# Attention and mixture-of-experts layer on one core: row scatters ahead of the sums of states in GpSimd's order, and one power instead of two for the second layernorm and the mean square

## The chip, the cores and the metric

The kernel runs on one core of a Trainium2 chip. Every time is device time in microseconds (us) of one execution. The engines of the core work side by side, each through its own instructions in its own order, and wait for one another by semaphores: TensorE (PE, matmuls, with PEld for its weight loads), VectorE (DVE), ScalarE (ACT), GpSimd (POOL), and SyncE (SP), which only issues transfers. The kernel is compared by the median time of its runs.

## The reference

The input x has 16 sequences of 512 tokens with 128 numbers each, all float32. Cut to what matters:

```python
q, k, v = silu(x @ Wq), silu(x @ Wk), x @ Wv            # 16 heads of 8
q, k = lrpe(q, theta), lrpe(k, theta)                   # [t*cos, t*sin]: 16 per head
energy = einsum('bhnd,bhmd->bhnm', q, k) * tril         # causal, no softmax
out = einsum('bhnm,bhmd->bhnd', energy, v) @ Wo
out = layernorm(out * sigmoid(x @ G1 @ G2)) * gamma + beta
x1 = layernorm(x + out)                                 # the second layernorm

xn = x1 * rsqrt(mean(x1 * x1) + eps)                    # the mean square, for the router only
probs = softmax(xn @ router_w.T)                        # 8 experts, the best 2 of each token
# each expert takes its first 1280 tokens: (silu(t @ rg) * (t @ ru)) @ rd, weighted, added back
ffn = silu(x1 @ sg) * (x1 @ su) @ sd + routed
return layernorm(x1 + ffn)
```

`x1` has variance var / (var + LN_EPS) over its 128 numbers and mean 0, where var is the variance before the second layernorm. So the mean square of `x1` follows from var alone, and both factors, (var + LN_EPS)^-0.5 and (var / (var + LN_EPS) + RMS_EPS)^-0.5, can be formed from it.

## The kernel before

**Layout.** Tokens lie on the 128 partitions. A chunk is 128 tokens; there are 64 chunks `t`, four to a sequence `b` (so `t = 4b + c`). Everything on PE, ACT, DVE and POOL runs in the order in which the program writes it: no engine takes an instruction ahead of another of its own.

**The first stage** (lines 788 to 832) is a loop over steps `t` = -2 to 64. Attention without softmax is computed by chunks with a running state, in a software pipeline. Step `t` emits, in this order:

- `project(t+2)`: one projection into the PSUM tile `pq` (L418, L421). ACT empties `pq` with SiLU into `qk` (L425, L427), tanh into `gate` (L433) and four copies into `vpad` (L441). DVE multiplies `qk` with cosines and sines into `hat` (L445).
- a piece of the shared feed-forward network of an earlier sequence, if one is ready: matmul `pg` (L137) and SiLU `sl` on ACT (L139), or matmul `pu` (L150) and product `h` on DVE (L151), or half of a down projection `pd` (L160) with a sum on DVE (L165).
- `turn_over(t+1)`: PE transposes `hat` into `pt` (L458); ACT copies it out as `kT`, `q2`, `qT` (L460 to L467). Another shared piece.
- `advance(turns)`: the next stage of `after(b)`, below.
- `energies(t)`: 32 small matmuls `pe` (L505), masked by four DVE products `et` (L513).
- `values(t-1)`: matmuls into `pout` from the states (L530) and from `et` (L538); ACT copies `pout` into `oT` (L544).
- `remember(t+1)`: matmuls `pst` (L479). DVE masks each into `add` (L488) and POOL adds it to the state (L490). A middle state and a last state come out of each chunk. They are read by `values` two and three steps later.
- if there are rows to send, up to two row scatters: first a tiny product `beat` on POOL (L740) which reads the `oT` column that ACT has just written, so that the scatter does not start before that; then one `scatter` (L723), an indirect DMA that GpSimd prepares, and a second one.
- `advance(turns)` again, then routing steps.

Most PSUM tiles of this stage come from one pool, `ps_w`, with four buffers in turn. A new tile takes the buffer of the tile four before it, so a matmul can wait for the engine that empties that older tile. The output projection `po` often takes the buffer of the `pq` that was filled in the same step.

**`after(b)`** finishes a sequence. It is a generator, and each `advance` runs it to its next `yield`, so its stages are half a step apart, or more: `po` (L553) and the POOL sum `x_sb + bet` (L554); the gate product `o` (L557); the first layernorm's statistics and its power `rstd` on POOL (L113); `w` in two stages (L565, L570); the statistics of `w` (L105, L107) and, with `rstd_of`, `ve = var + eps` on DVE (L111) and its power `r2` on POOL (L113); an empty stage; then `nb = -mean * r2` on DVE (L580), half of the normalised rows `x1` on ACT (L584, `normed_rows(0, 1)`), and for the mean square three small DVE operations on 128x4 numbers (L591, L592, L593) and a second power on POOL into `rms` (L594). Then follow the other half of the rows, their transpose, and the router's logits.

**Routing** runs three times (`route`, after sequences 5, 11 and 15). It reads `rms` and leaves 2 rows to scatter for each token chunk, 128 scatters in all. 52 of them go out in the loop, the others in the tail behind it (lines 838 to 856), each behind a `beat` on the newest `h`.

**The second stage** (lines 999 to 1066) runs the eight experts and the last layernorm. There POOL prepares only the scatters of the results (L934) and the powers of the last layernorm (L113).

Of the kernel before, what the change touches and what calls it, by code (L numbers as in the profile page):

```python
# [10 lines left out]
F32 = mybir.dt.float32  # L11
I32 = mybir.dt.int32
AF = mybir.ActivationFunctionType
ALU = mybir.AluOpType
# [5 lines left out]
P = 128  # L20
B, N, D = 16, 512, 128
NC = N // P
T = B * N
NT = T // P
# [5 lines left out]
LN_EPS = 1e-5  # L30
RMS_EPS = 2.0 ** -23
# [16 lines left out]
def tile_kernel(  # L48
# [20 lines left out]
    nc = tc.nc  # L69
# [20 lines left out]

    x1T = keep.tile([P, T], F32, name="x1T")
    base = x1T.rearrange("p (t d) -> p t d", d=D)
    rms = keep.tile([P, NT], F32, name="rms")
    logits = keep.tile([P, NT, E], F32, name="logits")
    idx = keep.tile([P, 2, NT], I32, name="idx")
    count = keep.tile([P, E], F32, name="count")
# [12 lines left out]
    def rstd_of(var, n, eps):  # L109
        ve = small.tile([P, n], F32, tag="ve", name="ve")  # L110
        nc.vector.tensor_scalar(ve, var, eps, None, ALU.add)  # L111
        r = small.tile([P, n], F32, tag="rstd", name="rstd")
        nc.gpsimd.tensor_tensor(r, ve, neghalf[:, :n], ALU.pow)  # L113
        return r
# [80 lines left out]
    with ExitStack() as ph:  # L195
# [351 lines left out]
        def after(b):  # L547

            mine = slice(b * NC, b * NC + NC)
            oT, gate, x_sb = oTs.pop(b), gates.pop(b), xs.pop(b)  # L550
            po = ps_w.tile([P, NC, D], F32, tag="w", name=f"po_{b}")
            for c in range(NC):
                nc.tensor.matmul(po[:, c, :], oT[:, ts(c, P)], wo_sb, start=True, stop=True)  # L553
            nc.gpsimd.tensor_tensor(x_sb, x_sb, bet.unsqueeze(1).to_broadcast([P, NC, D]), ALU.add)  # L554
            yield
            o = wk1.tile([P, NC, D], F32, tag="o", name=f"o_{b}")
            nc.vector.scalar_tensor_tensor(o, gate, 1.0, po, ALU.add, ALU.mult)  # L557
            yield
            mv = small.tile([P, NC, 2], F32, tag="mv", name="mv")
            ln_stats(o, mv, NC)  # L560
            r = rstd_of(mv[:, :, 1], NC, LN_EPS)
            yield
            w = wk1.tile([P, NC, D], F32, tag="w", name=f"w_{b}")
            for c in range(NC):
                nc.vector.scalar_tensor_tensor(  # L565
                    w[:, c, :], o[:, c, :], mv[:, c, 0:1], gam, ALU.subtract, ALU.mult
                )
            yield
            for c in range(NC):
                nc.vector.scalar_tensor_tensor(  # L570
                    w[:, c, :], w[:, c, :], r[:, c : c + 1], x_sb[:, c, :], ALU.mult, ALU.add
                )
            yield
            mv2 = small.tile([P, NC, 2], F32, tag="mv2", name="mv2")
            ln_stats(w, mv2, NC)
            r2 = rstd_of(mv2[:, :, 1], NC, LN_EPS)
            yield
            yield
            nb = small.tile([P, NC], F32, tag="nb", name="nb")
            nc.vector.scalar_tensor_tensor(nb, mv2[:, :, 0], -1.0, r2, ALU.mult, ALU.mult)  # L580

            def normed_rows(*chunks):
                for c in chunks:
                    nc.scalar.activation(  # L584
                        x1[:, b * NC + c, 0:D], w[:, c, :], AF.Identity, bias=nb[:, c : c + 1], scale=r2[:, c : c + 1]
                    )

            normed_rows(0, 1)

            sq = small.tile([P, NC], F32, tag="sq", name="sq")  # L590
            nc.vector.tensor_tensor(sq, r2, r2, ALU.mult)  # L591
            nc.vector.tensor_tensor(sq, sq, mv2[:, :, 1], ALU.mult)  # L592
            nc.vector.tensor_scalar(sq, sq, RMS_EPS, None, ALU.add)  # L593
            nc.gpsimd.tensor_tensor(rms[:, mine], sq, neghalf[:, :NC], ALU.pow)  # L594
            yield
            normed_rows(2, 3)
            yield
            px1 = ps_w.tile([P, N], F32, tag="w", name=f"px1_{b}")
            for c in range(NC):
                nc.tensor.transpose(px1[:, ts(c, P)], x1[:, b * NC + c, 0:D], ident)  # L600
            nc.scalar.copy(x1T[:, ts(b, N)], px1)
            yield "narrow"
            plg = ps_w.tile([P, P], F32, tag="w", name=f"plg_{b}")
            for c in range(NC):
                nc.tensor.matmul(
                    plg[32 * c : 32 * c + 32, :], rw_sb, x1T[:, ds(b * N + c * P, P)], start=True, stop=True
                )
            lg = wk1.tile([P, P], F32, tag="lg", name=f"lg_{b}")
            nc.scalar.copy(lg, plg)
            yield  # L610
            yield
            plt = ps_w.tile([P, NC, 32], F32, tag="w", name=f"plt_{b}")
            nc.tensor.transpose(plt.rearrange("p c e -> p (c e)"), lg, ident)
            nc.vector.tensor_copy(logits[:, mine, :], plt[:, :, 0:E])
            normed.add(b)
# [120 lines left out]
        def scatter_behind(column=None):  # L736

            if scatters:
                if column is not None:
                    nc.gpsimd.tensor_tensor(beat, column, neghalf[:, 0:1], ALU.mult)  # L740
                scatter(*scatters.pop(0))
# [6 lines left out]
        def advance(gens, slot=None):  # L748

            for g in list(gens):  # L750
                if told.get(id(g)) == slot:
                    told[id(g)] = next(g, gens)
                    if told[id(g)] is gens:
                        gens.remove(g)
                        del told[id(g)]
# [32 lines left out]
        with tc.manual_schedule(engines=ORDERED):  # L788
            for t in range(-2, NT + 1):
                coming, here, left = 0 <= t + 2 < NT, 0 <= t < NT, 0 <= t - 1 < NT  # L790
                stopped("wait")
                beginning(t)
                if coming:
                    if (t + 2) % NC == 0 and 2 <= (t + 2) // NC + 1 < B:
                        load_xT((t + 2) // NC + 1)
                        load_x((t + 2) // NC + 1)
                    project(t + 2)
                if t == 0:
                    nc.vector.tensor_scalar(wo_sb, wo_sb, 0.5, None, ALU.mult)
                if t == 2:  # L800
                    nc.sync.dma_start(sg_sb, sg)
                    nc.sync.dma_start(su_sb, su)
                    nc.sync.dma_start(sd_sb, sd.rearrange("(c p) d -> p c d", p=P))
                shared(t)
                sprinkle(t, 2)
                if 0 <= t + 1 < NT:
                    turn_over(t + 1)
                shared(t)
                advance(turns)
                if here:  # L810
                    energies(t)
                if stopped("exp"):
                    sprinkle(t, 1)
                if left:
                    values(t - 1)
                if 0 <= t + 1 < NT:
                    remember(t + 1)
                if left:

                    scatter_behind(oTs[(t - 1) // NC][:, ds((t - 1) % NC * P, 1)])  # L820
                    scatter_behind()
                advance(turns, "narrow")
                advance(turns)
                sprinkle(t, 3)
                beginning_done(t)
                if left and (t - 1) % NC == NC - 1:
                    b = (t - 1) // NC
                    turns.append(after(b))
                    ready[b] = t + (6 if b else 10)
                    for b0, b1 in groups:  # L830
                        if b == b1 - 1:
                            todo.append((b, route(b0, b1)))

            t, over, waited = NT + 1, 12, 0

            zero = vpads[0].rearrange("p a b d -> p (a b d)")[:, 0:N]
            nought(zero, N)
            while turns or todo or scatters or fills or over:
                if not (turns or todo or scatters or fills):
                    over -= 1  # L840
                shared(t)

                waited = waited + 1 if todo and told.get(id(todo[0][1])) == "wait" else 0
                if waited > 1:
                    stopped("wait")
                if stopped("exp"):
                    sprinkle(t, 1)
                if t % 2 == 0:
                    advance(turns, "narrow")
                    advance(turns)  # L850
                sprinkle(t, 3)
                if t % 2 == 0:
                    scatter_behind(latest[0])
                if t % 4 == 1 and fills:
                    fill(fills.pop(0))
                t += 1
# [256 lines left out]
```

## Time and profile before

| | us |
|---|---|
| median of 12 runs | 854.61 (852.68 to 857.12) |
| the profiled execution: its time | 854.15 |
| the profiled execution: span from first to last instruction | 852.4 |
| PE busy | 815.0 (96%) |
| DVE busy | 537.5 (63%) |
| ACT busy | 413.8 (49%) |
| POOL busy | 360.0 (42%) |
| POOL row scatters L723, 128 | 128.6, 1004 ns each |
| POOL powers L113, 45 | 48.6, 1080 ns each |
| POOL sums of states L490, 96 | 43.9, 458 ns each |
| POOL powers of the mean square L594, 16 | 16.6, 1040 ns each |

A row of the groups reads: line, engine, operation, output <- inputs, shapes, count, then busy time in all, mean ns of one, and the idle time of that engine just before them. A row of the timeline reads: start, duration (of all of the instructions merged into the row), engine, line, operation, tiles, and in brackets the idle time of the engine before it and who ended it. A row of the waits reads: who waited for whom, us in total, times, longest. Matmuls are pipelined and their ends are modelled, so a PE that is shown as busy can still lose a tenth of a microsecond between two matmuls; where that matters, starts are compared.

The first stage with its tail takes the span up to some 510 us. Within it the four chunks of a sequence take about 22 us, and in most of it PE shows no idle time, while DVE is busy for 17 to 18 us of each 22.

### The profile page before, as it was taken

The numbers are of one execution on the slowest core, as the hardware profiler recorded it, in microseconds if no ns is written. First come the engines' busy times: TensorE is split into PE (matmuls) and PEld (weight loads), VectorE is DVE, ScalarE is ACT, GpSimd is POOL, SyncE is SP. The second block draws the span as 40 slices with busy tenths as digits, with TensorE's granted clock in tenths as the row PEclk, the third lists the DMA queues.
The fourth block names the chain that finished last, engine by engine and source line by source line (L and its number), as shares of the span: only waits on it lengthen the run. The fifth ranks groups of instructions, "written<-read, shape, count | busy, mean of one in ns | idle before, by whom it ended". The sixth has DMA issues, their size and how long they took to land. (4 is left out here: it accounts for less than half of the span.)

```text
span 852.4 us, 25793 instructions
## 1 busy us (share of the span) xinstructions
PE 815.0 (96%) x10288; PEld 556.7 (65%) x10288; DVE 537.5 (63%) x1695; ACT 413.8 (49%) x1342; POOL 360.0 (42%) x512
## 2 busy tenths in 40 slices
PE   6899999989999999999999999999999999999996
PEld 4666667656766865755666666776777667765564
DVE  7688887889988788975433334443434443278864
ACT  5666776675676567534222221333333333323455
POOL 2233333322466776686766660433343333401110
PEclk9999999999999999999999999999999999999998
DMA  6011111110111110057000014213331110056512
GB/s 202 22 35 35 35 33 35 34 34 17 39 55 57 59 48 21 29 201 261 26 13 7 1 31 140 82 36 93 94 97 50 64 62 25 31 160 180 144 49 63
DMA packets 66395, 57.55 MB, mean 68 GB/s; under 512 B 6180, under 2 KB 55132, under 8 KB 66274
## 3 DMA queue, kind: packets, MB, share of 16 engines
q1 hardware_dynamic: 59474, 44.95, 17.2%
q0 software_dynamic: 6656, 10.69, 3.8%
q8 instruction: 81, 1.33, 0.6%
q14 instruction: 40, 0.33, 0.1%
q10 hardware_dynamic: 144, 0.26, 0.1%
HBM read 32.62 MB, written 26.48 MB: 69 GB/s over the span
## 5 line engine op out<-in xcount | busy, mean ns | idle before, releaser
L723 POOL DMA_INDIRECT xg_dram<-x,idx x128 | 128.6, 1004 | 40.5 <-issue 35.2
L934 POOL DMA_INDIRECT y_dram<-y,to x80 | 77.6, 970 | 158.0 <-ACT y L932 158.0
L151 DVE TENSOR_TENSOR h<-sl,pu 128x512 f32<-128x512 f32 x128 | 87.7, 685 | 84.6 <-PE pu L150 56.4
L139 ACT ACTIVATE sl<-pg 128x512 f32<-128x512 f32 x128 | 75.5, 593 | 118.1 <-PE pg L137 112.5
L150 PE MATMUL pu<-x1T,su_sb 128*128 128x512 f32 x256 | 130.9, 593 | 0.8 <-ACT sl L139 0.8
L137 PE MATMUL pg<-x1T,sg_sb 128*128 128x512 f32 x256 | 131.4, 595 | 0.0
L160 PE MATMUL pd<-sd_sb,h 128*128 128x128 f32 x1024 | 122.8, 276 | 4.4 <-DVE x1T L165 4.4
L1026 DVE TENSOR_TENSOR eh<-esl,peu 128x512 f32<-128x512 f32 (+1 forms) x96 | 57.5, 598 | 109.8 <-PE peu L1023 109.8
L160 PEld LDWEIGHTS pd<-sd_sb,h 128*128 128x128 f32 x1024 | 119.1, 192 | 11.2 <-issue 5.7
L113 POOL TENSOR_TENSOR rstd<-ve,neghalf 128x4 f32<-128x4 f32 x45 | 48.6, 1080 | 125.9 <-DVE ve L111 121.0
L928 PEld LDWEIGHTS ped<-rd,eh 128*128 128x128 f32 x640 | 84.0, 192 | 24.6 <-issue 22.5
L490 POOL TENSOR_TENSOR state<-state,add 128x128 f32<-128x128 f32 x96 | 43.9, 458 | 130.3 <-DVE add L488 127.7
L513 DVE TENSOR_TENSOR et<-pe,causal 128x256 f32<-128x256 f32 x256 | 90.2, 413 | 9.9 <-PE pe L505 9.8
L1021 PE MATMUL peg<-xgT,rg 128*128 128x512 f32 (+1 forms) x192 | 84.6, 522 | 0.0
L1023 PE MATMUL peu<-xgT,ru 128*128 128x512 f32 (+1 forms) x192 | 84.4, 521 | 0.0
L928 PE MATMUL ped<-rd,eh 128*128 128x128 f32 x640 | 84.3, 275 | 0.0
L1025 ACT ACTIVATE esl<-peg 128x512 f32<-128x512 f32 (+1 forms) x96 | 50.5, 526 | 55.0 <-PE peg L1021 52.3
L150 PEld LDWEIGHTS pu<-x1T,su_sb 128*128 128x128 f32 x256 | 45.7, 190 | 45.1 <-issue 39.0
L932 ACT ACTIVATE y<-ped,wt 128x128 f32<-128x128 f32 x80 | 29.4, 367 | 84.6 <-PE ped L928 84.6
L137 PEld LDWEIGHTS pg<-x1T,sg_sb 128*128 128x128 f32 x256 | 44.4, 191 | 36.9 <-issue 34.8
L418 PE MATMUL pq<-W,xT 128*128 128x384 f32 x128 | 61.0, 560 | 4.9 <-ACT qT L467 2.6
L445 DVE TENSOR_TENSOR hat<-qk,cst_tok 128x512 f32<-128x512 f32 x64 | 44.9, 702 | 26.5 <-ACT qk L427 26.4
(176 smaller groups left out, 1258.7 us busy)
## 6 DMA issues: line engine op xcount, KB each, us to landing
y_dram<-vpad SPq DMA_DIRECT2D x16, 512.0 KB, 7.0
y<-y_dram SPq DMA_DIRECT2D x32, 256.0 KB, 3.2
xT<-xt SPq DMA_DIRECT2D x15, 384.0 KB, 2.9
xg<-xg_dram SPq DMA_DIRECT2D x8, 660.0 KB, 4.4
x<-x SPq DMA_DIRECT2D x16, 256.0 KB, 3.3
o<-res SPq DMA_DIRECT2D x15, 256.0 KB, 2.3
xg_dram<-x,idx POOLq DMA_INDIRECT x128, 2.3
rg<-rg SPq DMA_DIRECT2D x8, 256.0 KB, 3.6
```

Source lines behind the costliest of these rows:

```text
L137: nc.tensor.matmul(pg, sg_sb[:, ts(i, P)], seq, start=True, stop=True)
L139: nc.scalar.activation(sl, pg, AF.Silu)
L150: nc.tensor.matmul(pu, su_sb[:, ts(i, P)], seq, start=True, stop=True)
L151: nc.vector.tensor_tensor(h[i // half][:, i % half, :], h.pop(("s", i)), pu, ALU.mult)
L160: nc.tensor.matmul(pd, h[k][:, i - k * half, ts(c, P)], sd_sb[:, i, :], start=(i == 0), stop=(i == IS // P - 1))
L418: nc.tensor.matmul(pq[:, :, 0:24], xts[b][:, c, 0:P], W[:, 0:384].rearrange("p (h n) -> p h n", n=24), start=True, stop=True)
L513: nc.vector.tensor_tensor(et.rearrange("p s i n -> p (s i) n"), pes[a, half].rearrange("p s i n -> p (s i) n"), causal.unsqueeze(1).to_bro ...
L723: i = nc.gpsimd.indirect_dma_start(out=xg_dram[:, :], out_offset=bass.IndirectOffsetOnAxis(ap=idx[:, k, t : t + 1], axis=0), in_=x1[:, t, ...
L928: nc.tensor.matmul(pd, h[:, i, ts(c, P)], got[e][2][:, i, :], start=(i == 0), stop=(i == IR // P - 1))
L934: i = nc.gpsimd.indirect_dma_start(out=y_dram[:, :], out_offset=bass.IndirectOffsetOnAxis(ap=to[:, at : at + 1], axis=0), in_=y, in_offset ...
L1021: nc.tensor.matmul(pg[:, :n], rg_sb[:, ts(i, P)], xgTs[e][:, ds(o0, n)], start=True, stop=True)
L1023: nc.tensor.matmul(pu[:, :n], ru_sb[:, ts(i, P)], xgTs[e][:, ds(o0, n)], start=True, stop=True)
```

## The change

Two things are changed.

1. In `after(b)` the second layernorm's stage forms both arguments at once: `ve[:, 0] = var + LN_EPS`, then `inv = 1 / ve[:, 0]`, `inv = inv * var`, `ve[:, 1] = inv + RMS_EPS`, on DVE, and one POOL power of 128x2x4 numbers writes both factors into the kept tile `norms`. `rms` is its second half. The three small DVE operations and the power that stood behind `nb` one step later are gone.
2. In the loop, the two scatters with their `beat` stand in front of `remember(t+1)` instead of behind it. PE, ACT, DVE and SP keep their order under this. On POOL the order of a step becomes `beat`, scatter, scatter, sums of states, instead of sums of states, `beat`, scatter, scatter.

```diff
-    rms = keep.tile([P, NT], F32, name="rms")
+    norms = keep.tile([P, 2, NT], F32, name="norms")
+    rms = norms[:, 1]
...
             ln_stats(w, mv2, NC)
-            r2 = rstd_of(mv2[:, :, 1], NC, LN_EPS)
+
+            ve = small.tile([P, 2, NC], F32, tag="ve2", name="ve2")
+            nc.vector.tensor_scalar(ve[:, 0], mv2[:, :, 1], LN_EPS, None, ALU.add)
+            inv = small.tile([P, NC], F32, tag="sq", name="inv")
+            nc.vector.reciprocal(inv, ve[:, 0])
+            nc.vector.tensor_tensor(inv, inv, mv2[:, :, 1], ALU.mult)
+            nc.vector.tensor_scalar(ve[:, 1], inv, RMS_EPS, None, ALU.add)
+            nc.gpsimd.tensor_tensor(
+                norms[:, :, mine], ve, neghalf[:, : 2 * NC].rearrange("p (k c) -> p k c", k=2), ALU.pow
+            )
+            r2 = norms[:, 0, mine]
             yield
             yield
...
             normed_rows(0, 1)
-
-            sq = small.tile([P, NC], F32, tag="sq", name="sq")
-            nc.vector.tensor_tensor(sq, r2, r2, ALU.mult)
-            nc.vector.tensor_tensor(sq, sq, mv2[:, :, 1], ALU.mult)
-            nc.vector.tensor_scalar(sq, sq, RMS_EPS, None, ALU.add)
-            nc.gpsimd.tensor_tensor(rms[:, mine], sq, neghalf[:, :NC], ALU.pow)
             yield
             normed_rows(2, 3)
...
                     values(t - 1)
+                if left:
+
+                    scatter_behind(oTs[(t - 1) // NC][:, ds((t - 1) % NC * P, 1)])
+                    scatter_behind()
                 if 0 <= t + 1 < NT:
                     remember(t + 1)
-                if left:
-
-                    scatter_behind(oTs[(t - 1) // NC][:, ds((t - 1) % NC * P, 1)])
-                    scatter_behind()
                 advance(turns, "narrow")
```

More of the change, by code (lines that the diff above doesn't have):

```diff
@@ L815, in tile_kernel @@
                     values(t - 1)
-                if 0 <= t + 1 < NT:
-                    remember(t + 1)
                 if left:
@@ L821, in tile_kernel @@
                     scatter_behind()
+                if 0 <= t + 1 < NT:
+                    remember(t + 1)
                 advance(turns, "narrow")
```

## The prediction

> **What bounds the kernel now.** I read the page's busy times first, then PE's waits, then the timeline of one sequence, then POOL's rows where the scatters run.
>
> ```profile
> PE 815.0 (96%) x10288; PEld 556.7 (65%) x10288; DVE 537.5 (63%) x1695; ACT 413.8 (49%) x1342; POOL 360.0 (42%) x512
> ```
>
> PE is the bound, POOL is far from it. So a cheaper POOL is worth nothing by itself; the change counts through what it does to PE's waits. Both moved parts lie in the first stage. What PE waits for there (who for whom, total us, times, longest), and what ACT waits for in front of the normalised rows:
>
> ```profile
> PE po L553 <- ACT vpad L441: 3.8, 2, 1.9
> PE pst L479 <- DVE h L151: 1.4, 2, 0.7
> ...
> ACT x L584 <- DVE nb L580: 23.2, 16, 2.4
> ```
>
> No PE wait names POOL. The output projection `po` waits for ACT's `vpad` copies, which empty the PSUM buffer that it takes; ACT does those behind the normalised rows L584; and these wait for `nb` on DVE once in each of the 16 sequences. The timeline of sequence 2 shows that chain:
>
> ```profile
> 92.31 0.17 DVE L111 TENSOR_SCALAR ve<-mv 128x4 f32<-128x4 f32 x1
> 92.39 0.69 DVE L445 TENSOR_TENSOR hat<-qk,cst_tok 128x512 f32<-128x512 f32 x1
> 92.99 0.68 DVE L151 TENSOR_TENSOR h<-sl,pu 128x512 f32<-128x512 f32 x1
> 93.59 1.41 DVE L513 TENSOR_TENSOR et<-pe,causal 128x256 f32<-128x256 f32 x4
> ```
>
> ```profile
> 94.92 0.48 DVE L488 TENSOR_TENSOR add<-pst,bmask 128x128 f32<-128x128 f32 x2
> ...
> 95.31 0.15 DVE L580 SCALAR_TENSOR_TENSOR nb<-mv,rstd 128x4 f32<-128x4 f32 x1
> 95.34 0.99 POOL L490 TENSOR_TENSOR state<-state,add 128x128 f32<-128x128 f32 x2 [1.39 <-DVE add L488]
> 95.38 0.43 DVE L591 TENSOR_TENSOR sq<-rstd 128x4 f32<-128x4 f32 x1
> ...
> 95.50 0.88 ACT L584 ACTIVATE x<-w,nb,rstd 128x128 f32<-128x128 f32 x2 [1.04 <-DVE nb L580]
> ...
> 96.71 1.02 PE L150 MATMUL pu<-x1T,su_sb 128*128 128x512 f32 x2
> 96.79 0.69 DVE L445 TENSOR_TENSOR hat<-qk,cst_tok 128x512 f32<-128x512 f32 x1 [0.43 <-ACT qk L427]
> 96.80 0.64 ACT L441 COPY vpad<-pq 64x64 f32<-64x64 f32 x4
> ...
> 97.57 0.86 PE L553 MATMUL po<-wo_sb,oT 128*128 128x128 f32 x6
> ```
>
> From `ve` at 92.31 to `nb` at 95.31 DVE has no bracket: it never waits, it is simply full. From `nb` on ACT is full: rows, `qk`, `gate`, `vpad` until 97.44, and `po` starts at 97.57, just when `pu` is through. So the cycle is balanced to a tenth of a microsecond here: PE is never idle, and DVE's queue between `ve` and `nb` has nothing to give. After `nb`, on the contrary, the three operations of the mean square (95.38 to 96.36) lie in DVE's wait for ACT; `hat` still waits 0.43 us behind them.
>
> **The three small operations (the first part of the change).** They leave the place behind `nb`, where the wait for `qk` hides them, so that gains nothing. They enter between `ve` and `hat`, where DVE is full. Price of one: undisturbed (sequence 15) the chain L591, L592, L593 starts at 385.37, 385.56 and 385.75, so 0.19 to 0.20 each with the wait for the result before. The reciprocal's nearest row is L121, 0.168 us on 128x4 and 128x1, with 0.03 of wait the same 0.20. Together 0.60. All that stands behind them on DVE comes 0.60 later: `hat`, `h`, the four `et`, the `add`s, `nb`; then the rows and `vpad` on ACT, then `po` on PE. What covers it, sequence by sequence, is a wait of DVE between `ve` and `nb`, or time by which `vpad` was done before `po` needed it. Where `po` visibly stalls it starts 0.05 after the last `vpad` copy (188.47 to 188.52), so cover is the distance less 0.05.
>
> - 0 and 1: `po` already waits, for DVE's `add` (starts 54.40 and 73.94, idle before it): 0.60 each.
> - 2, 3: `po` 0.13 behind `vpad`, cover 0.08: 0.52 each.
> - 4: DVE waits 0.16 for `pe`, cover at `po` 0.36: 0.08. 5: 0.20 and 0.26: 0.14.
> - 6 and 12: routing has switched ACT's table, PE idles 1.90 at `po` behind this very chain: 0.60 each.
> - 7 and 13: cover 0.08: 0.52 each.
> - 8, 9, 10 (scatters run): `nb` starts 0.03 to 0.07 behind the power and takes 0.42 instead of 0.15, beside a sum of states. Both go (next part): 0.30 to 0.34 back. With DVE's own waits (0.20 in 8, 0.32 in 10) that leaves 0.10, 0.26 and 0.
> - 11: waits 0.20 and cover 0.26: 0.14.
> - 14, 15: behind the loop PE runs on shared pieces: 0 from this.
>
> Sum 5.2 us. Nothing gives it back later: when PE stands, the next steps of all engines start from that later time, and the cycle was already limited by PE.
>
> **One power for two.** POOL loses 16 powers of 1.04 us, hidden before (PE never waits for POOL). The remaining power has 8 numbers a partition instead of 4; no row shows that. Lower end 1.04, as for 4. Upper end: a POOL product of one number (`beat`) takes 0.20, so four powers cost at most 0.85 above a floor of 0.19, and eight 1.89. A sum of 128 numbers takes only 0.46, so the 1.04 must lie in the power itself, by number; I take 1.89. Who waits: `nb`. In sequence 2 the power ends at 93.95 and `nb` starts at 95.31, and both move by 0.60, so 0.85 more fits. In 0 and 1 the distance is 0.76 and 0.77: 0.1 late each. In 14 `nb` waits for the power already (1.15 idle), and PE stands 0.77 at a `pu` behind it: 0.85 more. Sum 1.05; lower end 0.
>
> **The scatters in front of the sums.** In the 26 steps with scatters:
>
> ```profile
> 253.02 0.45 POOL L490 TENSOR_TENSOR state<-state,add 128x128 f32<-128x128 f32 x1 [2.26 <-DVE add L488]
> 253.44 0.19 POOL L740 TENSOR_TENSOR beat<-oT,neghalf 128x1 f32<-128x1 f32 x1
> 253.81 0.99 POOL L723 DMA_INDIRECT xg_dram<-x,idx  x1 [0.18 <-issue]
> 255.10 0.97 POOL L723 DMA_INDIRECT xg_dram<-x,idx  x1 [0.30 <-issue]
> 256.09 1.05 POOL L113 TENSOR_TENSOR rstd<-ve,neghalf 128x4 f32<-128x4 f32 x1
> 257.12 0.98 POOL L490 TENSOR_TENSOR state<-state,add 128x128 f32<-128x128 f32 x2
> ```
>
> POOL waited 2.26 for `add` while `oT` was there at 251.16. With the scatters first they run at about 251.6 to 253.8, the sum at 253.8, and the power of `r2` at `ve` plus three operations, about 254.8, instead of 256.09. That is why `nb` loses its wait in 8 to 10. The sums come up to 2.7 us later elsewhere (a `beat`, two scatters of 1.0 and their 0.3 gaps). What reads them, L530, runs two steps later: the sums of 257.12 end at 258.1 and are used by PE at about 267, a distance of 9 us. `add` has two buffers, each read a step before it is written again. The scatters' rows are read only after 508 us, in the experts' stage, and the tail's scatters are paced by `h`. SP's order is untouched, and the two indirect DMAs of a step are passed by nothing but the sums. So: no gain and no loss on PE, beyond the 0.3 counted above.
>
> One thing can go either way: DVE operations are longer beside POOL's sums, L591 takes 0.43 us there and 0.15 alone, and the second L565 of a sequence 0.57 instead of 0.34. Moved sums leave those and meet others (`w` L570, `hat`, the new product). Taken from both sides: 0.23 less or 0.28 more in each of five or six sequences, -1.2 to +1.7; as many meetings go as come, so 0.
>
> The Trainium skill, "SBUF — State Buffer", section "SBUF: two separate sides", says why, and speaks against this part: VectorE with two SBUF inputs and a GpSimd operation that reads SBUF exclude each other, and the later one stands until the earlier is through. The trace's 0.43 beside a sum agrees. By that rule alone a `hat` or product that comes just behind a sum could lose the sum's whole 0.46; six times that would be an estimate of 2.8 us more, where the rows give 0.
>
> **The sum.** 5.2 + 1.05 = 6.25 us more. Against the profiled execution, 854.15 (span 852.4 and 1.75 around it), that is 860.4; that execution lies 0.46 below the median of the runs, so 860.9 on the scale of the medians.
>
> **Rivals.** *Hidden:* the 0.60 vanishes because the chain has slack that starts and ends do not show, for instance where `vpad` is not what holds `po`. For it: PE shows idle time at `po` only a few times. Against it: the balance of 0.13 in sequences 2, 3, 7 and 13, and DVE without a wait for 3 us. Time: 854.6, or 855.7 with the power. *Faster, through the port:* sums behind the scatters leave DVE alone in its full stretch. Five L565 at 0.23 and three `nb` at 0.32 make 2.1 us less, 852.5. It decides only if the three operations cost under 0.15 us in each of 14 sequences, against 0.60 by the rows. *Larger:* the cover in 4, 5 and 8 to 11 isn't there, because the waits that give it come later too, and in 8 to 11 the sums meet the new operations: six sequences at 0.60 instead of 0.72 in all add 2.9, 863.8. For it: the sum at 253.8 would lie right on the new product. Against it: the waits for `pe` and `pu` that cover 4, 5, 8, 10 and 11 are PE's own.
>
> **How the numbers follow.** About 0.2% (1.7 us) is what a measurement here tells from no change. Forecast 0.64 (its own range 857 to 863), larger 0.18, hidden 0.10, faster 0.08. Slower 0.82, same 0.10, faster 0.08. The range leaves out hidden and faster (0.18) and takes in the partly hidden and the larger: 856.2 to 864.3.
>
> **What the profile after would show.** Right: three rows of about 0.17 us between `ve` and `hat`; `nb` some 3.5 us behind `ve` in sequences 2 and 3, where it is 3.0; PE's idle time before `po` above 3.8 us in total, with many more than two waits, all by `vpad`; the power of 8 at about 1.9 us; scatters starting some 2 us earlier in a step; `po` of sequence 3 about 22.6 us after that of sequence 2, not 22.1. Wrong: `po` at the same distance as before with the three operations in place (hidden), or `hat` and L570 stretched in the steps with scatters (larger).

## The result

The changed kernel takes 863.84 us (median; 862.10 to 865.42), and the kernel before, run beside it, 854.50 us. The ratio is 1.0109, with a 95% interval of 1.0097 to 1.0121: 9.3 us slower. The forecast was 860.9 us, with a range of 856.2 to 864.3. So the sign and the range held, and the size was 2.9 us short: 9.3 us more where 6.25 were forecast. The profiled execution of the changed kernel took 864.76 us with a span of 863.0.

### The profile page after: what moved, and what is told of

Same layout as the page of the kernel before. It is cut to its first block, busy times and chain, and to the rows that moved or that the text cites. A ratio compares the mean times of both kernels' runs of the same rounds, so it can differ in the third digit from the quotient of the medians.

```text
span 863.0 us, 25780 instructions
## 1 busy us (share of the span) xinstructions
PE 818.4 (95%) x10288; PEld 556.6 (64%) x10288; DVE 540.1 (63%) x1695; ACT 414.1 (48%) x1342; POOL 359.4 (42%) x496
## 3 DMA queue, kind: packets, MB, share of 16 engines
q8 instruction: 81, 1.33, 0.6%
## 5 line engine op out<-in xcount | busy, mean ns | idle before, releaser
L491 POOL TENSOR_TENSOR state<-state,add 128x128 f32<-128x128 f32 x96 | 46.8, 488 | 109.5 <-DVE add L489 106.6
L114 POOL TENSOR_TENSOR rstd<-ve,neghalf 128x4 f32<-128x4 f32 x29 | 30.7, 1057 | 120.3 <-DVE ve L112 120.3
L446 DVE TENSOR_TENSOR hat<-qk,cst_tok 128x512 f32<-128x512 f32 x64 | 51.2, 799 | 37.6 <-ACT qk L428 37.5
```

## The profile after

The busy times of the whole span come first, as on the page.

```profile
PE 818.4 (95%) x10288; PEld 556.6 (64%) x10288; DVE 540.1 (63%) x1695; ACT 414.1 (48%) x1342; POOL 359.4 (42%) x496
```

Sixteen POOL instructions are gone and DVE has as many as before. PE has the same matmuls in a longer span. The new time is in PE's waits. The chain's waits in the changed kernel (who for whom, total us, times, longest) are these:

```profile
PE po L554 <- ACT vpad L442: 5.7, 7, 1.9
...
PE pq L419 <- DVE h L152: 1.9, 2, 1.0
PE pq L419 <- DVE x1T L166: 1.8, 2, 0.9
PE po L554 <- DVE add L489: 1.6, 2, 0.8
...
ACT x L595 <- DVE nb L591: 32.7, 16, 3.2
```

`po` now waits for `vpad` seven times, 5.7 us in all, where it was twice and 3.8. `po` also waits for `add` on DVE, 1.6 us in two waits, where it was 0.4 in one. ACT waits 32.7 us for `nb`, 9.5 more than before: 0.59 a sequence on average. The waits of `pq` for `h` and for `x1T` have grown from 0.3 and 0.5 us to 1.9 and 1.8: there PE is held by DVE directly, without the rows and `vpad` between them.

The timeline of sequence 2 (start, duration, engine, line, operation; in brackets the idle time before it) shows where the 0.60 us goes. The `po` behind the `nb` of a sequence is that of the next one; as in the prediction, it is counted here to the sequence of the `nb`.

```profile
93.89 0.17 DVE L583 TENSOR_SCALAR ve<-inv 128x4 f32<-128x4 f32 x1
93.96 0.68 DVE L446 TENSOR_TENSOR hat<-qk,cst_tok 128x512 f32<-128x512 f32 x1
94.14 2.02 POOL L584 TENSOR_TENSOR norms<-ve,neghalf 128x8 f32<-128x8 f32 x1 [1.41 <-DVE ve L583]
...
96.89 0.15 DVE L591 SCALAR_TENSOR_TENSOR nb<-mv,norms 128x4 f32<-128x4 f32 x1
...
97.07 0.88 ACT L595 ACTIVATE x<-w,nb,norms 128x128 f32<-128x128 f32 x2 [1.65 <-DVE nb L591]
...
98.37 1.30 DVE L446 TENSOR_TENSOR hat<-qk,cst_tok 128x512 f32<-128x512 f32 x1 [1.33 <-ACT qk L428]
98.38 0.64 ACT L442 COPY vpad<-pq 64x64 f32<-64x64 f32 x4
99.07 1.16 PE L554 MATMUL po<-wo_sb,oT 128*128 128x128 f32 x8 [0.37 <-ACT vpad L442]
```

The first `ve` of this sequence (L579) starts at 93.27, three small operations follow, and only then comes `hat`. From `ve` to `nb` it is 3.61 us, where it was 3.00. The power of eight numbers ends at 96.16 and `nb` starts at 96.89, so the power is not what `nb` waits for here. `nb`, rows and `vpad` come 0.6 later, and `po`, which stood for nothing before, now stands 0.37. From `po` of this sequence to `po` of the next it is 22.71 us (99.07 to 121.78), where it was 22.09 (97.57 to 119.66). Behind `nb`, where the three operations used to lie, DVE simply waits longer for `qk`: 1.33 instead of 0.43. That is time freed where nobody needs it. The `hat` behind it takes 1.30, where it took 0.69: it now lies on POOL's sum `x_sb + bet`, which no second power holds back any more. PE shows no wait for it in this sequence.

## The experiments

The first four kernels ran on a chip on which the kernel before takes 854.93. The second four (866.88) and the last four (866.04) ran on two other chips; that difference is taken up at the end, and each ratio is against the kernel before on the same chip.

### First part alone

The new mean square and the one power of eight, with the sums still in front of the scatters:

```diff
-            r2 = rstd_of(mv2[:, :, 1], NC, LN_EPS)
+            ve = small.tile([P, 2, NC], F32, tag="ve2", name="ve2")
+            nc.vector.tensor_scalar(ve[:, 0], mv2[:, :, 1], LN_EPS, None, ALU.add)
+            inv = small.tile([P, NC], F32, tag="sq", name="inv")
...
+            nc.gpsimd.tensor_tensor(
+                norms[:, :, mine], ve, neghalf[:, : 2 * NC].rearrange("p (k c) -> p k c", k=2), ALU.pow
+            )
+            r2 = norms[:, 0, mine]
...
-            sq = small.tile([P, NC], F32, tag="sq", name="sq")
...
-            nc.gpsimd.tensor_tensor(rms[:, mine], sq, neghalf[:, :NC], ALU.pow)
```

> The kernel before with the first part alone: three small operations early, one power of 8, the scatters behind the sums as before. Place theory (three DVE operations in the full stretch between ve and nb cost up to 0.6 us a sequence): the 5.2 us of the forecast stay; where scatters run, the power starts only after them, about 256.1, and ends 0.2 us behind the time at which nb could start, so sequences 8 to 10 lose their cover; with the power's 1.05 that makes 7 to 8 us more than before. Order theory (the changed order on POOL costs the 3 us by which the change came out above the forecast): not over 6.5 us more, and well below the whole change.

Measured: 863.49 us, ratio 1.0109 (1.0086 to 1.0131), 8.6 us more by the medians and 9.3 by the ratio. The first part by itself costs as much as the whole change, so the missing 3 us are not the price of the order alone, which would have left at most 6.5 here. The profile also shows what the second part saves in the sequences with scatters. Here, in sequence 8, the power stands behind two scatters:

```profile
235.44 0.98 POOL L727 DMA_INDIRECT xg_dram<-x,idx  x1 [0.30 <-issue]
236.42 1.71 POOL L583 TENSOR_TENSOR norms<-ve,neghalf 128x8 f32<-128x8 f32 x1
```

```profile
238.16 0.42 DVE L590 SCALAR_TENSOR_TENSOR nb<-mv,norms 128x4 f32<-128x4 f32 x1 [0.35 <-POOL norms L583]
```

```profile
240.61 1.16 PE L554 MATMUL po<-wo_sb,oT 128*128 128x128 f32 x8 [0.56 <-ACT vpad L442]
```

`nb` waits 0.35 for the power, takes 0.42 instead of 0.15 beside a sum, and `po` stands 0.56. By the starts of the same matmuls, sequences 8, 9 and 10 cost 0.51, 0.81 and 0.29 here and 0.06, 0.42 and -0.10 in the changed kernel. So the second part does give 1.2 us back there, and takes it again later (below).

### Second part alone

```diff
                 if left:
                     values(t - 1)
-                if 0 <= t + 1 < NT:
-                    remember(t + 1)
                 if left:
                     scatter_behind(oTs[(t - 1) // NC][:, ds((t - 1) % NC * P, 1)])
                     scatter_behind()
+                if 0 <= t + 1 < NT:
+                    remember(t + 1)
                 advance(turns, "narrow")
```

> The kernel before with the second part alone: scatters ahead of the sums, the mean square in its old place with its own power. Place theory: within 0.1% of before, -0.5 to +1 us: nb loses its wait in three sequences, some hat are longer beside the sums. Order theory: 2.5 to 3.5 us slower than before.

Measured: 855.02 us, ratio 1.0003 (0.9990 to 1.0017): nothing, within -0.9 and +1.5 us. The term of 0 held as a sum, but not because nothing happens. By the starts of the matmuls, PE loses 0.53 in sequence 12 and 0.36 in 13. In 12, for example, the product `prob` takes 0.67 instead of 0.35 beside the moved sum, and `pq` stands 0.68 for `h`, where it was 0.04. And PE gains 0.1 each in 8 and 10 and 0.35 at the `pu` behind the loop.

### The three operations early, two powers of four

```diff
-            r2 = rstd_of(mv2[:, :, 1], NC, LN_EPS)
+            ve = small.tile([P, 2, NC], F32, tag="ve2", name="ve2")
+            nc.vector.tensor_scalar(ve[:, 0], mv2[:, :, 1], LN_EPS, None, ALU.add)
+            r2 = small.tile([P, NC], F32, tag="rstd", name="rstd")
+            nc.gpsimd.tensor_tensor(r2, ve[:, 0], neghalf[:, :NC], ALU.pow)
+            inv = small.tile([P, NC], F32, tag="sq", name="inv")
+            nc.vector.reciprocal(inv, ve[:, 0])
+            nc.vector.tensor_tensor(inv, inv, mv2[:, :, 1], ALU.mult)
+            nc.vector.tensor_scalar(ve[:, 1], inv, RMS_EPS, None, ALU.add)
...
-            sq = small.tile([P, NC], F32, tag="sq", name="sq")
-            nc.vector.tensor_tensor(sq, r2, r2, ALU.mult)
-            nc.vector.tensor_tensor(sq, sq, mv2[:, :, 1], ALU.mult)
-            nc.vector.tensor_scalar(sq, sq, RMS_EPS, None, ALU.add)
-            nc.gpsimd.tensor_tensor(rms[:, mine], sq, neghalf[:, :NC], ALU.pow)
+            nc.gpsimd.tensor_tensor(rms[:, mine], ve[:, 1], neghalf[:, :NC], ALU.pow)
```

> The kernel before with nothing but the three small operations moved in front of hat; two powers of 4 at their old places. Place theory: 5.2 us more than before, 859.7, since the place alone makes the cost. Power theory (nb comes late because the power of 8 is longer): no change.

Measured: 859.57 us, ratio 1.0054 (1.0039 to 1.0070), 4.6 us more (3.3 to 6.0). This is the place of the three operations and nothing else: POOL has the powers of before, at their old places. Expected were 5.2. The profiled execution, 862.08, is the slowest of five; by the starts of its matmuls PE loses 6.1 us to waits. PE's waits in this kernel:

```profile
PE po L553 <- ACT vpad L441: 4.9, 5, 1.9
...
PE po L553 <- DVE add L488: 1.5, 2, 0.8
```

The waits by `vpad` rise from two to five with the three operations alone.

### The power of eight alone

```diff
-            r2 = rstd_of(mv2[:, :, 1], NC, LN_EPS)
+            ve = small.tile([P, 2, NC], F32, tag="ve2", name="ve2")
+            nc.vector.tensor_scalar(ve, mv2[:, :, 1].unsqueeze(1).to_broadcast([P, 2, NC]), LN_EPS, None, ALU.add)
+            both = small.tile([P, 2, NC], F32, tag="rstd2", name="rstd2")
+            nc.gpsimd.tensor_tensor(both, ve, neghalf[:, : 2 * NC].rearrange("p (k c) -> p k c", k=2), ALU.pow)
+            r2 = both[:, 0]
```

> The kernel before with a first power of 8 numbers instead of 4 (the second four are copies that nothing reads); the mean square as before. Power theory: most of the change's 9.3 us. Place theory: the power is longer by 0.85; nb waits for it only in sequences 0, 1 (0.1 each), 8 to 11, where it starts behind the scatters (0.6 to 0.8 each) and 14 (0.85): 3 to 4 us more than before.

Measured: 857.39 us, ratio 1.0031 (1.0019 to 1.0044), 2.5 us more, a little under the 3 to 4 expected of the place theory. By the profile the delay arises in five places: 0.53, 0.63 and 0.51 at `po` of sequences 8, 9 and 11, where the longer power stands behind the scatters, 0.63 in sequence 14, and 0.20 at the start of the experts' stage. The theory that the longer power is the cause of the whole change falls: it had expected most of 9.3. But the price forecast for it, 1.05, was too low as well.

The two halves of the first part make 4.6 + 2.5 = 7.1, and together they cost 8.6; the difference of 1.5 is no larger than the intervals of the three ratios allow.

### Twice the small operations

The changed kernel with three more operations, copies of the three, behind L583.

```diff
+            spare = small.tile([P, 3, NC], F32, tag="spare", name="spare")
+            nc.vector.reciprocal(spare[:, 0], ve[:, 1])
+            nc.vector.tensor_tensor(spare[:, 1], spare[:, 0], mv2[:, :, 1], ALU.mult)
+            nc.vector.tensor_scalar(spare[:, 2], spare[:, 1], RMS_EPS, None, ALU.add)
```

> The changed kernel with three more such small operations behind the three, on numbers that nothing reads. Place theory: another 0.6 us in each of the 14 or so sequences, and the covers of the forecast are used up, so the added cost is nearly full: 7.5 to 9.5 us over the changed kernel, 871 to 873. Order and power theories: the same time as the changed kernel, to 1 us.

Measured: 875.97 us, ratio 1.0108 (1.0089 to 1.0128), on a chip where the kernel before takes 866.88. On the third chip, where it takes 866.04, the changed kernel takes 869.25 (below). So three more operations cost about 6.7 us by the medians, 6.1 by the ratios; the comparison is across two chips. That is a little under the 7.5 expected at least, and more than the first three cost alone (4.6). The starts of the matmuls in this kernel and in the changed one of the third chip show why: eleven sequences now cost 0.59 to 0.68 each, 5, 8, 9 and 11 among them, so the cover is used up there; 4 and 10 still cost only 0.06 and 0.01. In sequence 2 `nb` moves by the same step again, from 3.61 to 4.23 us behind `ve`. DVE's share of the span is 63% all the while.

### Taking out the chain from `nb` to `po`: the rows one stage later

The kernel before, with all four blocks of rows put where the second two were. So `vpad` stands in front of them in ACT's order.

```diff
-            normed_rows(0, 1)
...
             yield
-            normed_rows(2, 3)
+            normed_rows(0, 1, 2, 3)
             yield
```

> The kernel before with all four blocks of normalised rows half a step later, behind turn_over, so that ACT's copies of pq no longer stand behind nb. If nb, rows, vpad, po is the chain that holds PE, its idle time at po goes: 1.9 us each in sequences 6 and 12, some 0.6 in others, and with it a piece of slow clock behind such a stall: 3 to 5 us faster than before. If the chain is not what holds PE: no change, or slower, since oT is then copied behind four blocks instead of two.

Measured: 863.59 us where the kernel before takes 866.88, ratio 0.9962 (0.9949 to 0.9975).

The same edit of the changed kernel:

> The changed kernel with the same later rows. Place theory with the chain through rows and vpad: a large part of the cost of the three operations is then covered; what stays is where PE waits for DVE directly (add in sequences 0 and 1, h and x1T beside routing in 6, 7, 12, 13) and the longer power in 14: 3 to 5 us over the kernel before with later rows, instead of 9.3. If the cost goes another way than through nb: 9 us over it.

Measured: 858.87 us, ratio 0.9916 (0.9899 to 0.9932). That is 4.7 us under the kernel before with late rows, not 3 to 5 over it; the order of the scatters differs between the two (below).

PE's waits by `vpad` in the kernel before with late rows fall from 3.8 us to this:

```profile
PE pout L538 <- issue: 6.7, 18, 0.5
...
PE po L553 <- ACT vpad L441: 0.9, 2, 0.5
```

That is the chain as the prediction read it, as far as `po` goes: with `vpad` ahead of the rows, `po` hardly waits. The first of the two lines is a different thing, found only on these chips, and told of at the end.

### `nb` in front of the masks

Scatters first and the old mean square, with `nb` and two rows put ahead of the masks of the sums, so that `nb` no longer stands behind the `add`s.

```diff
-            yield
+            yield "nb"
             nb = small.tile([P, NC], F32, tag="nb", name="nb")
...
             normed_rows(0, 1)
+            yield
...
+                advance(turns, "nb")
                 if 0 <= t + 1 < NT:
                     remember(t + 1)
```

> Scatters first, the mean square in its old place, and nb with two blocks of rows emitted ahead of the sums' masks, so 0.4 us earlier on DVE. If the chain holds PE: 0.4 us in sequences 6 and 12 and up to 0.1 in others are gained, 0.1 each in 0 and 1 lost: 0.5 to 1.5 us faster than with the scatters first alone. If not: the same.

Measured: 854.80 us where the kernel before takes 866.88, ratio 0.9863 (0.9847 to 0.9880). PE's two long waits, in sequences 6 and 12, shrink from 1.90 to 1.51 each, as expected. This kernel also has the scatters first, which on this chip is worth something by itself, so the whole 12 us can't be put down to `nb`.

### The same on a third chip, and the best of both

The changed kernel again, and the two kernels with late rows again:

> The changed kernel itself, beside the kernels with later rows. In the call before, the kernel before ran at 866.9 where it had been 854.5 to 854.9, and in the trace of the later rows PE stood 18 times for 0.4 us at pout without a visible cause, each time with a scatter's packets in flight. If that belongs to the chip of that call: where the kernel before is at 854 to 855 here, the changed one is 9 to 10 us over it. If it is a state that a kernel falls into: the distance can be anything.

> The kernel before with the rows half a step later, once more. If the stalls at pout belong to the chip of the call before and the kernel before is at 854 to 855 here: none of them, 4 to 6 us faster than before, 849 to 851. If they come from the order of this kernel: again about 18 stalls and 3 us or less gained.

> The changed kernel with later rows, once more, now beside both of its neighbours. Place theory with the chain through rows and vpad: 3 to 5 us over the kernel before with later rows, and 7 us or more under the changed kernel. If the cost does not go through nb: 9 us over the former.

Measured, where the kernel before takes 866.04: the changed kernel 869.25, ratio 1.0038 (1.0025 to 1.0051); the kernel before with late rows 863.94, ratio 0.9969 (0.9958 to 0.9980); the changed kernel with late rows 858.40, ratio 0.9902 (0.9887 to 0.9918). So the late rows take 10.9 us off the changed kernel. The last expectation, that the changed kernel with late rows would stay 3 to 5 us above the kernel before with late rows, was missed again: it is 5.5 below. The two also differ in the order of the scatters, which counts on these chips (last section), so the comparison does not isolate the mean square.

The kernel that isolates it has scatters first, late rows and the old mean square. In the last sequence the rows stay where they were.

```diff
-            normed_rows(0, 1)
+            if b == B - 1:
+                normed_rows(0, 1)
...
-            normed_rows(2, 3)
+            normed_rows(*((2, 3) if b == B - 1 else (0, 1, 2, 3)))
```

> Scatters first, the mean square in its old place, and the rows half a step later in all sequences but the last: a version meant to beat both kernels. If the chain over nb, rows and vpad holds PE, it has the gain of the later rows on every chip: 4 to 6 us faster than before where that is at 854 to 855, more where it is at 866. If not: the same as before.

Measured: 852.14 us, ratio 0.9838 (0.9822 to 0.9853). It beats both kernels: 13.9 us under the kernel before and 17.1 under the changed one on that chip. Part of that is the order of the scatters, which counts on this chip. Its timeline in sequence 2 (the lines around `po`) shows what the late rows do:

```profile
92.87 0.15 DVE L580 SCALAR_TENSOR_TENSOR nb<-mv,rstd 128x4 f32<-128x4 f32 x1
...
93.71 0.65 ACT L441 COPY vpad<-pq 64x64 f32<-64x64 f32 x4
...
95.13 1.05 PE L553 MATMUL po<-wo_sb,oT 128*128 128x128 f32 x8
...
96.11 1.68 ACT L584 ACTIVATE x<-w,nb,rstd 128x128 f32<-128x128 f32 x4
```

`vpad` no longer follows `nb` through the rows: it ends 0.77 us ahead of `po`, and the four rows run behind `po`.

Against this kernel, the changed kernel with late rows is 6.3 us slower (858.40 to 852.14). Its scatters stand the same, and its rows too but for the last sequence. So even with the path through `vpad` out of the way, most of the price of the new mean square stays. By the starts of the matmuls, sequences 2 and 3, where that path was the whole price, cost nothing any more (-0.53 and -0.32); 6, 7, 12 and 13 still cost 0.61, 0.62, 0.75 and 0.64. Its profile shows where PE then waits:

```profile
PE pq L419 <- DVE h L152: 1.9, 2, 1.0
...
PE pq L419 <- DVE x1T L166: 1.7, 2, 0.9
PE po L554 <- DVE add L489: 1.6, 2, 0.8
```

These are the direct waits of the changed kernel, unchanged: `h`, `x1T` and `add` stand behind the three operations on DVE, and PE waits for them without ACT.

## Why the prediction was right, and where it was short

The delay of PE that the change adds, sequence by sequence, is read from the starts of the same matmuls in the two traces (stretches at half the clock taken out). Beside it stand the terms of the prediction. The two spans differ by 10.6; what is beyond 9.06 lies ahead of sequence 0 and in the clock.

| sequence | forecast us | in the profile us |
|---|---|---|
| 0, 1 | 0.70, 0.70 | 0.62, 0.72 |
| 2, 3 | 0.52, 0.52 | 0.55, 0.62 |
| 4, 5 | 0.08, 0.14 | 0.09, 0.06 |
| 6, 7 | 0.60, 0.52 | 0.72, 0.73 |
| 8, 9, 10 | 0.10, 0.26, 0 | 0.06, 0.42, -0.10 |
| 11 | 0.14 | 0.72 |
| 12, 13 | 0.60, 0.52 | 0.94, 0.93 |
| 14 | 0.85 | 1.42 |
| start of the experts' stage | 0 | 0.56 |
| sum | 6.25 | 9.06 |

**The place of the three operations: right.** 0.60 was the price, and 0.61 to 0.62 is the distance that `nb` moved in sequences 0 to 3, 6, 7, 12 and 13. The covers named for 4, 5, 8 and 10 exist: these four cost 0.11 together, where 0.32 was forecast. As a term, 5.2 was forecast; the kernel that has this edit alone takes 4.6 more by its median and loses 6.1 in its profiled run, so 5.2 lies between.

But in sequences 6, 7, 12 and 13, which carry 2.24 of the 5.2, only the size was right, and the path was another. The prediction put their cost at `po`, behind `nb`, the rows and `vpad`. Sequence 12, before and then changed, PE alone:

```profile
323.54 0.91 PE L418 MATMUL pq<-W,xT 128*128 128x384 f32 x2
...
328.73 1.16 PE L553 MATMUL po<-wo_sb,oT 128*128 128x128 f32 x8 [1.90 <-ACT vpad L441]
```

```profile
327.83 0.91 PE L419 MATMUL pq<-W,xT 128*128 128x384 f32 x2 [0.98 <-DVE h L152]
...
333.02 1.25 PE L554 MATMUL po<-wo_sb,oT 128*128 128x128 f32 x6 [1.90 <-ACT vpad L442]
```

The wait of 1.90 at `po` is the same as before, in 6 as in 12. PE loses its time earlier, at `pq`: it stands for `h` 0.88 in 6 (0.26 before) and 0.98 in 12 (0.04 before), and for `x1T` 0.92 in 7 (0.30 before) and 0.91 in 13 (0.23 before). `h` and `x1T` come behind the three operations on DVE like `nb`, and so they too come about 0.6 later. That is why the size agrees, and why the late rows do not give this part back. With the three operations alone the four waits are 0.87, 0.68, 0.91 and 0.85. The sign "all by `vpad`" failed here and in 0 and 1, where `po` waits for `add`.

**The range: in part luck.** 863.84 lies above the 857 to 863 that the prediction gave for its own account. It lies in the whole range because that took in the rival called larger, and it meets the 863.8 of that rival almost exactly. But the first reason of that rival, that the cover in 4, 5, 8 and 10 is gone, did not come true.

**The order of the scatters: right alone as a sum, not in company.** Alone it is worth 0.0003 of the time, as forecast (0), with the losses in 12 and 13 named above. The waits and the 0.42 of `nb` in 8 to 10 went, as forecast: `nb` takes 0.15 everywhere. But beside the new operations the meetings do not balance. Sequence 11 of the changed kernel shows it, on DVE and then on POOL:

```profile
301.32 0.57 DVE L579 TENSOR_SCALAR ve<-mv 128x4 f32<-128x4 f32 x1
301.93 0.18 DVE L581 RECIPROCAL inv<-ve 128x4 f32<-128x4 f32 x1
302.14 0.28 DVE L582 TENSOR_TENSOR inv<-inv,mv 128x4 f32<-128x4 f32 x1
302.45 0.17 DVE L583 TENSOR_SCALAR ve<-inv 128x4 f32<-128x4 f32 x1
302.53 0.68 DVE L446 TENSOR_TENSOR hat<-qk,cst_tok 128x512 f32<-128x512 f32 x1
```

```profile
300.92 0.97 POOL L728 DMA_INDIRECT xg_dram<-x,idx  x1 [0.30 <-issue]
301.91 0.47 POOL L491 TENSOR_TENSOR state<-state,add 128x128 f32<-128x128 f32 x1
```

`ve` takes 0.57 instead of 0.17 and ends as the scatter's issue does, and the product takes 0.28 instead of 0.16 beside the moved sum. From `ve` to `hat` it is 1.21 us, where it was 0.07. The cover of 0.46 that the prediction named here (0.20 and 0.26) is used up, and `po` stands 0.48:

```profile
306.93 0.85 DVE L446 TENSOR_TENSOR hat<-qk,cst_tok 128x512 f32<-128x512 f32 x1 [1.33 <-ACT qk L428]
...
307.41 1.21 POOL L491 TENSOR_TENSOR state<-state,add 128x128 f32<-128x128 f32 x2
307.63 1.16 PE L554 MATMUL po<-wo_sb,oT 128*128 128x128 f32 x8 [0.48 <-ACT vpad L442]
```

This is the second half of the rival called larger (the sums meet the new operations). In 11 to 13 the change costs 2.59 where 1.26 was forecast; the three operations alone cost 1.47 there (0.08, 0.75, 0.64), so about 1.1 comes with the order and the power. Against the first part alone, the second part gives 1.2 us back in 8 to 10, and takes 0.31 in sequence 12, 0.29 in 13, 0.72 in 14 and 0.17 at the start of the experts' stage: 1.5 us. Hence the sum near zero.

**On the rule weighed in the prediction.** The trace agrees in kind with the exclusion of which the Trainium skill tells in "SBUF — State Buffer", section "SBUF: two separate sides": in the changed kernel `hat` lengthens to 0.85 to 0.99 us in six scatter steps where it lies on a sum, and the sum at 307.41 takes 1.21 for two where two take 0.99 otherwise. Here both of the two that meet are longer, the product and the sum. The estimate by that rule alone was 2.8 us; the second part alone costs 0.1 (at most 1.5 by its interval), so for that part the rows decided rightly.

**One power for two: the term that was mis-sized.** The duration was right: 1.88 us, where 1.89 was taken.

```profile
L584 POOL TENSOR_TENSOR norms<-ve,neghalf 128x8 f32<-128x8 f32 x16 | 30.1, 1880 | 16.1 <-DVE ve L583 16.1
```

Its price of 1.05 was not. Measured alone it costs 2.5, of which some 1.7 lies in 8, 9 and 11, where the scatters hold the power back; the changed kernel avoids that in 8 by its order, and only in part in 9 and 11. In sequence 14 it was put at 0.85, and PE's stand at `pu` grows from 0.77 to 1.25; with what follows, that is 0.59. The other 0.83 of that sequence arises ahead of `pu`, part of it where `po` now stands 0.14 for `h`; with the first part alone it is 0.11, so it takes both parts together. There the sentence "14, 15: 0 from this" failed. By the medians the place and the order make 4.7 of the 9.3, and 4.6 are left for the power and the company of the parts; by the profiled runs it is 9.06 less 6.1, about 3.0. In either reading 1.05 was too little.

**The start of the experts' stage: not forecast.** PE waits there for `x1T`, 1.31 us before and 1.86 after. First the kernel before, then the changed one, PE alone:

```profile
518.57 2.05 PE L160 MATMUL pd<-sd_sb,h 128*128 128x128 f32 x16 [1.31 <-DVE x1T L165]
```

```profile
527.06 2.92 PE L161 MATMUL pd<-sd_sb,h 128*128 128x128 f32 x16 [1.86 <-DVE x1T L166]
```

The wait grows by 0.56 here, by 0.39 with the first part alone, by 0.32 with the operations alone and by 0.20 with the power alone; why it grows there, long after them, stays open. In the profiled run it also brings a stretch of half clock: the same 16 matmuls take 2.92 instead of 2.05 and the next group 1.86 instead of 1.02, about 1.7 us.

**The other rivals.** Hidden would have needed `po` at its old distance; it moved from 22.09 to 22.71. Faster through the port would have needed the second part to gain 2 us alone; it gained none.

## What to carry to other kernels

Price an operation by the place in the queue that it enters: on an engine that is 63% busy, 0.6 us of small operations cost their full length in every sequence where that stretch of the queue was full and the bound engine stood at its end, and nothing behind it, where the engine waited anyway. Then ask why the bound engine's buffer is emptied behind a late operand at all: moving the rows behind the copies that empty it took 2.1 and 3.3 us off the kernel before on the two other chips, while the 16 powers that GpSimd lost could give nothing, since PE never waited for GpSimd. And look for every wait of the bound engine on the delayed queue, not only for the longest: here about a third of the delay came through `pq`, which had waited at most 0.3 us for the same `h` and `x1T` before. Where two parts of a change share an engine's queue, measure them together too: alone they cost 8.6 and 0.1, but the one took back what the other gave in some places and added to it in others.

## What was not expected of the hardware

**The chips differ, and the scatters' order matters on some.** The kernel before takes 854.5 to 854.9 us in its own runs and on the chip of the first four experiments, and 866.9 and 866.0 on the two others. There, the kernel before itself was not profiled. The kernel before with late rows was, once on each of the two, and it has the sums in front of the scatters too: its traces show 18 and 19 stalls of PE at `pout`, up to 0.5 us each and 6.7 us together in each trace, with no engine named ("issue" above). They go with the scatters: in the first of the two traces, 14 of the 18 begin between 0.1 us ahead of the end of a step's second scatter on GpSimd and 0.3 behind it (228.69 to 229.11, for example, where the scatter lasts from 227.79 to 228.76). The packets of that scatter move only later, from 229.34 on; the other four stalls lie on packets of a step's first scatter. So it is not, as one expectation has it, that packets are in flight each time. The kernels with the scatters first show only 3 or 4 of them there; the changed kernel on the third chip:

```profile
PE pout L539 <- issue: 1.5, 4, 0.5
```

In the profiles of the first chips, of either order, there is no such row. So the second part of the change, worth nothing on the one kind of chip (1.0003), avoids about 5 us of stalls on the other, and that is in line with the change costing 1.09% on the one and 0.38% on the other. The second part alone was not run on such a chip, and what in the chip makes the difference stays open: the stalls, and one wait of PE at `pg` of 1.6 to 2.0 us between 497 and 520 us that seven of the eight kernels profiled there show, would account for most of the 11 to 12 us, not for all.

**The clock can be halved after a wait of 1.9 us.** The granted clock by stretches, in the changed kernel (us; busy time of PE, weight loads, DVE, ACT, POOL; granted clock; DMA share and GB/s):

```profile
328.00:335.00 7.00, 5.10 (x36) 3.25 (x44) 4.04 (x11) 5.35 (x17) 4.20 (x6) 0.89 0.06 19
335.00:341.00 6.00, 6.00 (x120) 3.83 (x104) 4.84 (x12) 3.36 (x14) 2.65 (x5) 0.84 0.06 18
...
528.00:534.00 6.00, 5.42 (x23) 3.63 (x22) 1.69 (x4) 0.60 (x1) 0.00 (x0) 0.72 0.09 22
```

Both places are behind waits of PE of 1.9 us (at `po` of sequence 12, and at `pd`), and at each the clock is halved for about 3.4 us: the last row loses 0.28 of 6 us, 1.7 us, which is half of 3.4, and the first two rows together lose 1.7 as well. The Trainium skill, "TensorE: Matmul & The Clock Gate", Part 1, tells of windows of about 3.4 us and of half the rate after an idle one; the length agrees, but here a wait of 1.9 us was enough. It does not come each time, and it comes without such a wait too. The kernel before has such a stretch behind the wait of sequence 6 and none behind that of 12, and another from 59.2 on (granted clock 0.92 from 58 to 80 us), shortly behind waits of 0.94 and 0.47. The kernel with the scatters first alone has both waits of 1.90 at `po` and no such stretch between 31 and 846 us. At `pd` it goes with the length: four profiled kernels wait there 1.84 to 1.98 and have it, the ten others wait 1.18 to 1.70 and have none. A wait of that length thus costs more than itself in some runs: about 1.7 us in the case at `pd`.
